# A cross-attention and quantized-GLU kernel whose instruction order comes from a planner: a margin for TensorE in the plan, four planned durations, and new due times

## The chip, the cores and the metric

The kernel runs on one core of a Trainium2 chip. The metric is the device time of one execution in microseconds (us); three runs of the kernel before gave 574.42, 576.3 and 575.2 us, median 575.2. A core has engines with an instruction stream each: TensorE (PE in the profile; its weight loads are PEld), VectorE (DVE), ScalarE (ACT), GpSimd (POOL) and SyncE (SP), which here issues all DMAs. The streams run side by side and meet only in semaphores, so an engine that waits holds up everything behind it in its own stream.

## The reference, cut to what matters

There are 8 batches of 512 rows with 256 features, and a context of 64 rows for each.

```python
def block(x, ctx):                       # x (8, 512, 256), ctx (8, 64, 256), float32
    y = normalized(x)
    y = layernorm(y + attention(y, y, y, causal=True), g1, beta1)
    y = layernorm(y + attention(y, ctx, ctx, causal=False), g2, beta2)
    h = relu(y @ w1 + b1)                # 256 -> 1024
    y = layernorm(y + h @ w2 + b2, g3, beta3)
    x = x + y
    z = fp4(normalized(x))               # blocks of 16, scale = max |.| / 6, grid 0 .. 6
    h = silu(z @ fp4(w_gate).T) * (z @ fp4(w_up).T)     # 256 -> 704
    return x + fp4(h) @ fp4(w_down).T
```

## The kernel before, in words

The work of a batch has five stages: self-attention (`self_attention`, stage 0), cross-attention (`cross_attention`, 1), the MLP (`mlp`, 2), gate and up products of the GLU (`glu`, 3) and its quantization and down product (`down` in `glu`, 4). Rows are tiled by 128, so a batch has four row tiles. Everything is in float32; a TensorE product therefore shows twice the number of matmul instructions.

The functions do not emit instructions. They call `plan.op(engine, cost, emit, reads, writes, ...)` with a planned duration in us and the buffers that the operation reads and writes. When all batches are described, `Plan.order` (line 192) plays a small list schedule: each of the five engines takes, whenever it is free in the plan, the ready operation with the smallest key, and the sequence found in this way is what is emitted, engine by engine. The plan's times are not in the program; only the order is.

- A key is the latest start that still meets a due time (`_keys`, line 153): the table `DUE` gives one due for each batch and stage, the nine rows being batches 0 to 7 and the constants' loads (columns, index -1). An operation takes the minimum of its own due and of the latest starts of all that follow it, less the hop (`HOP`, `NEXT`) and its cost. TensorE's operations of a batch are also chained to each other.
- `push` is added to a key. Loads of x and z get `-LOAD_EARLY`; the preparation of the quantized weights (`weights`) gets a large positive one. That preparation is described with batch 0 and stage 0, as are the loads of w1 and w2.
- An operation counts as ready when its last input has landed and a hop has passed, 0.25 us behind TensorE, 0.13 behind VectorE, 0.16 behind ScalarE.
- Buffers come from kinds with a number of homes (`plan.kind`) or a share of another kind's homes (`plan.share` with a quota). An operation that needs a home waits in the plan until one is free; in an ordered kind homes are given in the order of description.

Transposes go by TensorE and a ScalarE copy for the first batches (`BY_PRODUCTS`: 4, 2 and 1 batches for the three uses in `turned`), else by a split into 16-bit planes on ScalarE, a store to device memory and a transposing DMA (`turned_by_transfers`). `down` transposes by DMA too, but by TensorE in the last batch.

The lines that the steps below speak of: L358 and L366 load x and z; L448, L438, L439, L458 and L465 are a normalisation's statistics (VectorE) and power (GpSimd), L524 its result on ScalarE; L480, L488, L496, L503 are the statistics of the norms by sums, where L488 are the squares on ScalarE, each with an accumulator read behind it; L537 and L545 apply such a norm on VectorE. L419 are transposes on TensorE, L831 the copy of their result (turned) on ScalarE, L767 the causal scores, L778 their exponentials, L787 the causal select on GpSimd, L800 the causal products with the values, L806 and L807 the division. In cross-attention L867 copies the context's transpose (zT), L883 makes the keys' products, L896 copies them (kq), L900 turns them, L927 is the product with the values. L961 and L981 are the MLP's two products, L969 the relu between them. L1036 is gate and up, L1048 and L1055 silu and the product, L578 to L610 the fp4 quantization, L1071 the split into planes, L1116 the down product, L1126 the addition to x and L1133 the store. L743 loads the norms' vectors, L729 b1 (c_rows), L1149 writes the pads, L1156 and L1160 load w1 and w2. L381 clears part of hqT, L378 sets a column of z, both on GpSimd ahead of everything.

Of the kernel before, what the change touches and what calls it, by code (L numbers as in the profile page):

```python
# [19 lines left out]
P = 128  # L20
# [12 lines left out]
PE_PASS = 0.429 / 512  # L33
HOP = {"PE": 0.25, "DVE": 0.13, "ACT": 0.16, "POOL": 0.1, "SP": 0.1}

NEXT = {"PE": 0.0, "DVE": 0.11, "ACT": 0.11, "POOL": 0.0, "SP": 0.0}
TABLE = 1.29

# [2 lines left out]
TILED = 2.65  # L41

BY_PRODUCTS = (4, 2, 1)
LOAD_EARLY = 2191.0
DUE = [
    [-1877.0, 638.0, 1236.0, -86.0, 359.0],
    [-498.0, 1140.0, 299.0, -53.0, 352.0],
    [251.0, 920.0, -109.0, 452.0, 665.0],
    [2244.0, 599.0, -92.0, 754.0, 95.0],
    [1032.0, 759.0, 1302.0, 1127.0, 22.0],  # L50
    [818.0, -579.0, 119.0, -1108.0, 586.0],
    [771.0, -1583.0, 341.0, 621.0, 85.0],
    [127.0, -388.0, -430.0, -94.0, -1479.0],
    [-2334.0],
]


# [31 lines left out]
class Plan:  # L89
# [102 lines left out]
    def order(self):  # L192
        self._keys()
        now, events, tick = 0.0, [], 0
        waiting = {e: [] for e in HOP}
        free_at = dict.fromkeys(HOP, 0.0)
        table, out = None, []
        for o in self.ops:
            o.left, o.ready = len(o.pred), 0.0
            if not o.left:  # L200
                waiting[o.engine].append(o)
        running = {}
        while True:
            progress = True
            while progress:
                progress = False
                for e in HOP:
                    if free_at[e] > now:
                        continue
                    best = None  # L210
                    for o in waiting[e]:
                        if o.ready > now:
                            continue
                        switch = o.table is not None and o.table != table
                        rank = (o.key + (4.0 if switch else 0.0), o.serial)
                        if (best is None or rank < best[0]) and self._take(o, False):
                            best = (rank, o, switch)
                    if best is None:
                        continue
                    _, o, switch = best  # L220
                    self._take(o, True)
                    waiting[e].remove(o)
                    if o.table is not None:
                        table = o.table
                    end = now + o.cost + (TABLE if switch else 0.0)
                    free_at[e] = end
                    out.append((now, o))
                    landed = end + o.lag
                    heapq.heappush(events, (end, tick, "end", None))
                    heapq.heappush(events, (landed, tick, "landed", o))  # L230
                    tick += 1
                    for s in o.succ:
                        s.left -= 1
                        s.ready = max(s.ready, landed + (NEXT if s.engine == e else HOP)[e])
                        if not s.left:
                            waiting[s.engine].append(s)
                            heapq.heappush(events, (s.ready, tick, "ready", s))
                            tick += 1
                    progress = True
            if not events:  # L240
                break
            now = events[0][0]
            while events and events[0][0] <= now:
                _, _, what, o = heapq.heappop(events)
                if what == "landed":
                    heapq.heappush(events, (now + HOP[o.engine], tick, "free", o))
                    tick += 1
                elif what == "free":
                    for b in o.bufs:
                        b.users -= 1  # L250
                        if not b.users:
                            k = self.kinds[b.kind]
                            k["free"].append(b.home)
                            k["held"] -= 1
        assert len(out) == len(self.ops), "the plan does not end"
        self.span = now
        return out
# [3 lines left out]
def kernel(  # L261
# [22 lines left out]
    SZ = z.shape[1]  # L284
# [20 lines left out]
    def several(name, count, shape):  # L305
        return [fixed(f"{name}_{k}", shape) for k in range(count)]


    plan = Plan(due=DUE)
    plan.kind("x", several("x", 6, [P, NT, D]))  # L310

    y0_homes = several("y0", 2, [P, NT, D + 2])

    z_homes = several("z", 8, [P, D + 2])
    plan.kind("y0", y0_homes)
    plan.kind("z", z_homes)
    plan.kind("zT", several("zT", 6, [P, ND, SZ]))
    plan.kind("turned", several("turned", 3, [P, ND, S]), ordered=False)
    plan.share("y0T", "turned", 1)
    plan.share("yT", "turned", 3, ordered=False)  # L320
    plan.share("zqT", "turned", 3)
    plan.kind("e", several("e", 1, [P, NT * (NT + 1) // 2 * P]))
    plan.kind("r", several("r", 3, [P, NT, D]))
    plan.kind("kq", several("kq", 4, [P, S // 2]))
    plan.kind("xp", several("xp", 6, [P, NT, SZ]))
    plan.kind("xpT", several("xpT", 3, [P, NT // 2 * P]))
    plan.kind("hT", several("hT", 8, [P, S]))
    plan.kind("zq", several("zq", 1, [P, NT, D]))
    plan.kind("zm", several("zm", 2, [P, NT * D]), ordered=False)
    plan.kind("wide", several("h", 8, [P, NI * P]), ordered=False)  # L330
    plan.share("h", "wide", 5)
    plan.share("hm", "wide", 3)
    plan.share("wq", "wide", 7)
    hqT_homes = several("hqT", 3, [P, NI * P])
    plan.kind("hqT", hqT_homes)

    hd_homes = [dram.tile([P, 2, NI * P], U16, tag=f"hd_{k}", name=f"hd_{k}") for k in range(3)]
# [2 lines left out]
    plan.kind("rest", [rest_home])  # L340
    zd_homes = [dram.tile([NT, P, 2, D], U16, tag=f"zd_{k}", name=f"zd_{k}") for k in range(4)]
    plan.kind("zd", zd_homes, ordered=False)
    plan.kind("ln", several("ln", 12, [P, 48]), ordered=False)
    plan.kind("q", several("q", 6, [P, 3, 64]), ordered=False)
    plan.kind("rt", several("rt", 7, [P, 4]), ordered=False)
    banks = [psum.tile([P, 512], F32, tag=f"bank{k}", name=f"bank_{k}") for k in range(8)]
    plan.kind("bank", banks, ordered=False)

# [76 lines left out]
    def norm_stats(v, view, pairs):  # L425

        s = plan.buf("ln")

        def st(t):
            return s.ap[:, 6 * t : 6 * t + 6]  # L430

        def mv(t):
            return s.ap[:, 24 + 2 * t : 26 + 2 * t]

        def variances(ts_):
            lo, hi = ts_[0], ts_[-1] + 1
            for t in ts_:
                nc.vector.bn_aggr(mv(t), st(t))  # L438
            nc.vector.tensor_scalar(  # L439
                s.ap[:, 32 + lo : 32 + hi],  # L440
                s.ap[:, 24:32].rearrange("p (t k) -> p t k", k=2)[:, lo:hi, 1], EPS, None, ALU.add,
            )

        for ts_ in pairs:
            lo, hi = ts_[0], ts_[-1] + 1
            for t in ts_:
                plan.op(
                    "DVE", 0.33, lambda t=t: nc.vector.bn_stats(st(t), view(t)),  # L448
                    reads=[(v, t)], writes=[(s, ("st", t))],
                )  # L450
            plan.op(
                "DVE", 0.1 + 0.09 * len(ts_), lambda ts_=ts_: variances(ts_),
                reads=[(s, ("st", t)) for t in ts_],
                writes=[(s, ("var", lo))] + [(s, t) for t in ts_],
            )
            plan.op(
                "POOL", 1.05,
                lambda lo=lo, hi=hi: nc.gpsimd.tensor_tensor(  # L458
                    s.ap[:, 36 + lo : 36 + hi], s.ap[:, 32 + lo : 32 + hi], mhalf[:, lo:hi], ALU.pow
                ),  # L460
                reads=[(s, ("var", lo))], writes=[(s, ("rstd", t)) for t in ts_],
            )
            plan.op(
                "DVE", 0.15,
                lambda lo=lo, hi=hi: nc.vector.scalar_tensor_tensor(  # L465
                    s.ap[:, 40 + lo : 40 + hi],
                    s.ap[:, 24:32].rearrange("p (t k) -> p t k", k=2)[:, lo:hi, 0],
                    -1.0, s.ap[:, 36 + lo : 36 + hi], ALU.mult, ALU.mult,
                ),
                reads=[(s, ("rstd", t)) for t in ts_] + [(s, t) for t in ts_],  # L470
                writes=[(s, ("shift", t)) for t in ts_],
            )
        return s

    def sums_stats(v, view, s):
# [8 lines left out]
        )  # L484
        for t in range(NT):
            plan.op(
                "ACT", 0.52,
                lambda t=t: nc.scalar.activation(  # L488
                    squares, view(t), AF.Square, bias=s.ap[:, 24 + t : 25 + t],
                    accum_out=s.ap[:, 28 + t : 29 + t],  # L490
# [8 lines left out]
            reads=[(s, ("sq", t)) for t in range(NT)], writes=[(s, "var")],  # L499
        )  # L500
        plan.op(
            "POOL", 1.05,
            lambda: nc.gpsimd.tensor_tensor(s.ap[:, 36:40], s.ap[:, 32:36], mhalf, ALU.pow),  # L503
            reads=[(s, "var")], writes=[(s, ("rstd", t)) for t in range(NT)],
        )
# [241 lines left out]
    def self_attention(b, xs):  # L747
# [13 lines left out]
        for k in range(NT):  # L761
# [3 lines left out]
            def scores(k=k, n=n, sc=sc):  # L765
# [17 lines left out]
            )  # L783

            plan.op(
                "POOL", 0.35,
                lambda k=k: nc.gpsimd.affine_select(  # L787
                    out=e.ap[:, ds(start[k], P)], in_=e.ap[:, ds(start[k], P)],
                    compare_op=ALU.is_ge, fill=0.0, base=0, pattern=[[1, P]],
# [157 lines left out]
    def mlp(b, r, xs):  # L947
# [8 lines left out]
        for f in range(NF):  # L956
            hp, h = plan.buf("bank"), plan.buf("hT")

            def product(f=f, hp=hp):
# [5 lines left out]

            plan.op("PE", ND * pe(S), product, reads=[yT, ready["w1"]], writes=[hp], takes=[h])
            plan.op(
                "ACT", act(S, True),
                lambda f=f, hp=hp, h=h: nc.scalar.activation(  # L969
                    h.ap, hp.ap, AF.Relu, bias=b1_sb[:, f : f + 1]  # L970
                ),
# [188 lines left out]
        "SP", 5.2, lambda: nc.sync.dma_start(w2_sb, w2.rearrange("(c p) d -> p c d", p=P)),  # L1160
        writes=[ready["w2"]],
    )
    plan.push = 2035.0
    weights()
    plan.push = 0.0
    for b in range(B):
# [38 lines left out]
```

## Time and profile before

| What | Value |
|---|---|
| Median of 3 runs | 575.2 us (574.42 to 576.3) |
| The profiled execution, its own time | 576.26 us |
| Its span, first to last instruction | 574.5 us |
| Mean granted clock of TensorE | 1.000 |
| Costliest on TensorE: L1036, 512 matmuls | 157.5 us |
| L981, 512 matmuls | 112.6 us |
| L961, 256 matmuls | 112.5 us |
| L1116, 384 matmuls | 87.2 us |
| VectorE's costliest: L603 on h, 76 | 66.8 us |
| ScalarE's costliest: L488 on r, 96 | 48.7 us, 508 ns each |
| DMA traffic | 66.88 MB, mean 116 GB/s |

The page names an engine's busy time and its share of the span, then draws the span in 40 slices of 14.4 us, each digit a busy share in tenths (9 is 90% or more). The waits view adds up who waited for whom: the total, how often, the longest. The chain of work goes back from the last instruction to what released each step; in order of time a line is start, length, and what ran. A timeline line is start, duration, engine, line, operation, out<-in, shapes, count. Durations that overlap in an engine's pipeline are longer than the distance of two starts.

### The profile page before, as it was taken

The numbers are of one execution on the slowest core, as the hardware profiler recorded it, in microseconds if no ns is written. First come the engines' busy times: TensorE is split into PE (matmuls) and PEld (weight loads), VectorE is DVE, ScalarE is ACT, GpSimd is POOL, SyncE is SP. The second block draws the span as 40 slices with busy tenths as digits, with TensorE's granted clock in tenths as the row PEclk, the third lists the DMA queues.
The fourth block names the chain that finished last, engine by engine and source line by source line (L and its number), as shares of the span: only waits on it lengthen the run. The fifth ranks groups of instructions, "written<-read, shape, count | busy, mean of one in ns | idle before, by whom it ended". The sixth has DMA issues, their size and how long they took to land.

```text
span 574.5 us, 7037 instructions
## 1 busy us (share of the span) xinstructions
PE 563.8 (98%) x2209; PEld 391.2 (68%) x2209; DVE 447.8 (78%) x1125; ACT 361.8 (63%) x761; POOL 62.2 (11%) x93
## 2 busy tenths in 40 slices
PE   5999999999999999999999999999999999999997
PEld 2767584866747668658486667766765866877686
DVE  4789988869998865755259999978997656399892
ACT  4677869598887672791638558887845256364431
POOL 3521101011200120110101102210100000010000
PEclk9999999999999999999999999999999999999999
DMA  7770387246466513322023546585771421436501
GB/s 236 119 230 2 101 219 169 73 119 157 116 158 175 137 52 83 99 71 49 1 73 98 137 126 156 148 198 154 153 180 62 124 62 38 111 106 151 151 19 46
DMA packets 143220, 66.88 MB, mean 116 GB/s; under 512 B 107976, under 2 KB 142672, under 8 KB 143184
## 3 DMA queue, kind: packets, MB, share of 16 engines
q1 hardware_dynamic: 143184, 66.44, 45.4%
q8 instruction: 17, 0.28, 0.2%
q14 instruction: 19, 0.16, 0.1%
HBM read 10.42 MB, written 29.66 MB: 70 GB/s over the span
## 4 chain that ended last, share of the span: by engine, by line
PE 98%; ACT 1%; DMA 0%; SPq 0%; issue 0%; DVE 0%; ACTq 0%
PE bank L1036 27%; PE bank L981 19%; PE bank L961 19%; PE bank L1116 15%; PE bank L767 7%; PE bank L800 6%; PE bank L419 2%; PE bank L927 1%; PE bank L883 1%; DMA z<-in_ctx_dram 0%; ACT squares L488 0%; PE bank L900 0%; SPq L358 0%; ACT turned L831 0%; PE bank L1102 0%
## 5 line engine op out<-in xcount | busy, mean ns | idle before, releaser
L1036 PE MATMUL bank<-wgu,turned 128*128 128x352 f32 x512 | 157.5, 460 | 0.0
L1036 PEld LDWEIGHTS bank<-wgu,turned 128*128 128x128 f32 x512 | 96.3, 190 | 51.8 <-issue 1.7
L981 PE MATMUL bank<-w,hT 128*128 128x256 f32 x512 | 112.6, 379 | 0.0
L961 PE MATMUL bank<-turned,w 128*128 128x512 f32 x256 | 112.5, 593 | 0.0
L981 PEld LDWEIGHTS bank<-w,hT 128*128 128x128 f32 x512 | 97.0, 190 | 13.8
L1116 PE MATMUL bank<-wd,hqT 128*128 128x256 f32 x384 | 87.2, 380 | 0.0
L961 PEld LDWEIGHTS bank<-turned,w 128*128 128x128 f32 x256 | 48.2, 190 | 56.9 <-issue 51.7
L1116 PEld LDWEIGHTS bank<-wd,hqT 128*128 128x128 f32 x384 | 72.4, 190 | 14.2 <-issue 2.9
L503 POOL TENSOR_TENSOR ln<-ln,mhalf 128x4 f32<-128x4 f32 x32 | 37.7, 1180 | 352.0 <-DVE ln L496 352.0
L603 DVE SCALAR_TENSOR_TENSOR h<-h,h 128x704 f32<-128x704 f32 (+2 forms) x76 | 66.8, 883 | 3.8 <-ACT h L597 3.4
L488 ACT ACTIVATE squares<-r,ln 128x256 f32<-128x256 f32 x96 | 48.7, 508 | 32.0 <-DVE ln L480 29.7
L969 ACT ACTIVATE hT<-bank,cols 128x512 f32<-128x512 f32 x64 | 42.8, 681 | 21.7 <-PE bank L961 21.5
L1048 ACT ACTIVATE h<-bank 128x352 f32<-128x352 f32 x64 | 29.2, 460 | 36.4 <-PE bank L1036 32.5
L1071 ACT COPY h<-h 128x1408 uint16<-128x1408 uint16 x28 | 38.0, 1362 | 19.4 <-DVE h L610 17.9
L1055 DVE TENSOR_TENSOR h<-h,bank 128x352 f32<-128x352 f32 x64 | 32.4, 516 | 12.3 <-PE bank L1036 8.6
L992 DVE SCALAR_TENSOR_TENSOR r<-bank,r 128x256 f32<-128x256 f32 x32 | 13.5, 421 | 35.0 <-PE bank L981 34.7
L767 PE MATMUL bank<-turned 128*128 128x512 f32 (+3 forms) x128 | 39.8, 457 | 0.4 <-ACT turned L831 0.4
L597 ACT ACTIVATE h<-h 128x704 f32<-128x704 f32 (+2 forms) x38 | 29.7, 788 | 14.0 <-DVE h L591 13.9
L800 PE MATMUL bank<-y,e 128*128 128x258 f32 x160 | 36.8, 381 | 0.0
L800 PEld LDWEIGHTS bank<-y,e 128*128 128x128 f32 x160 | 30.1, 190 | 5.9 <-issue 1.0
L591 DVE SCALAR_TENSOR_TENSOR h<-h,q 128x704 f32<-128x704 f32 (+2 forms) x38 | 33.5, 883 | 0.2
L610 DVE TENSOR_TENSOR h<-h,q 128x704 f32<-128x704 f32 (+2 forms) x38 | 33.4, 879 | 0.2
(90 smaller groups left out, 639.9 us busy)
## 6 DMA issues: line engine op xcount, KB each, us to landing
zd<-zm SPq DMA_DIRECT2D x25, 512.0 KB, 3.0
hd<-h SPq DMA_DIRECT2D x30, 352.0 KB, 3.0
out_dram<-x SPq DMA_DIRECT2D x32, 128.0 KB, 1.7
x<-in_x_dram SPq DMA_DIRECT2D x7, 512.0 KB, 5.3
w<-in_L_xattn_w_dram SPq DMA_DIRECT2D x2, 1024.0 KB, 7.4
z<-in_ctx_dram SPq DMA_DIRECT2D x16, 64.0 KB, 4.6
zd<-h SPq DMA_DIRECT2D x2, 384.0 KB, 3.1
h<-in_L_ffn_w_down_dram SPq DMA_DIRECT2D x2, 352.0 KB, 4.2
```

The costliest lines, as they stand in the source:

```text
L488: lambda t=t: nc.scalar.activation(squares, view(t), AF.Square, bias=s.ap[:, 24 + t : 25 + t], accum_out=s.ap[:, 28 + t : 29 + t],),
L503: lambda: nc.gpsimd.tensor_tensor(s.ap[:, 36:40], s.ap[:, 32:36], mhalf, ALU.pow),
L591: lambda: nc.vector.scalar_tensor_tensor(blocks_of(view()), blocks_of(view()), TIE, each(rc()), ALU.mult, ALU.mult),
L603: lambda reverse=reverse, f=f: nc.vector.scalar_tensor_tensor(view(), mm(), LEAST, view(), ALU.max, f, reverse1=reverse),
L767: nc.tensor.matmul(sc.ap[:, :n], yT.ap[:, c, ts(k, P)], yT.ap[:, c, k * P :], start=(c == 0), stop=(c == ND - 1),)
L800: nc.tensor.matmul(av.ap[:, : D + 2], e.ap[:, ds(start[k] + (t - k) * P, P)], y0.ap[:, k, :], start=(k == 0), stop=(k == t),)
L961: nc.tensor.matmul(hp.ap, w1_sb[:, c, ts(f, P)], yT.ap[:, c, :], start=(c == 0), stop=(c == ND - 1),)
L969: lambda f=f, hp=hp, h=h: nc.scalar.activation(h.ap, hp.ap, AF.Relu, bias=b1_sb[:, f : f + 1]),
L981: nc.tensor.matmul(fp.ap[:, :D], hT[f].ap[:, ts(t, P)], w2_sb[:, f, :], start=(f == 0), stop=(f == NF - 1),)
L1036: nc.tensor.matmul(gp.ap[:, :HI], zT.ap[:, c, ts(t, P)], wgu[:, c, ds(j * I + n * HI, HI)], start=(c == 0), stop=(c == ND - 1),)
L1071: lambda: nc.scalar.copy(planes(), h.ap[:, :I].bitcast(U16).rearrange("p (k h) -> p h k", h=2)),
L1116: nc.tensor.matmul(op.ap[:, :D], hqT.ap[:, ts(c, P)], wd[:, c, :], start=(c == 0), stop=(c == NI - 1),)
```

## The change

In the plan, an operation of TensorE whose input comes from another engine counts as ready 0.3 us later than before (`MARGIN`). Four planned durations are others: a square on ScalarE 0.63 for 0.52, the relu `act(S) + 0.08` = 0.57 for `act(S, True)` = 0.68, the power on GpSimd 1.12 for 1.05, the causal select 0.44 for 0.35. The due times of all batches, LOAD_EARLY and the weights' push have new values, and some kinds have another number of homes: x 5 for 6, z 7 for 8, zT 7 for 6, xp 3 for 6, xpT 6 for 3, hT 9 for 8, hqT 4 for 3, ln 11 for 12, rt 6 for 7; y0T may hold 3 of the turned homes for 1, wq 8 of the wide ones for 7. What is computed, and with which instructions, stays.

```diff
--- before.py
+++ after.py
@@ -33,6 +33,8 @@
 PE_PASS = 0.429 / 512
 HOP = {"PE": 0.25, "DVE": 0.13, "ACT": 0.16, "POOL": 0.1, "SP": 0.1}
 
+MARGIN = 0.3
+
 NEXT = {"PE": 0.0, "DVE": 0.11, "ACT": 0.11, "POOL": 0.0, "SP": 0.0}
 TABLE = 1.29
 
@@ -41,17 +43,17 @@
 TILED = 2.65
 
 BY_PRODUCTS = (4, 2, 1)
-LOAD_EARLY = 2191.0
+LOAD_EARLY = 1700.0
 DUE = [
-    [-1877.0, 638.0, 1236.0, -86.0, 359.0],
-    [-498.0, 1140.0, 299.0, -53.0, 352.0],
-    [251.0, 920.0, -109.0, 452.0, 665.0],
-    [2244.0, 599.0, -92.0, 754.0, 95.0],
-    [1032.0, 759.0, 1302.0, 1127.0, 22.0],
-    [818.0, -579.0, 119.0, -1108.0, 586.0],
-    [771.0, -1583.0, 341.0, 621.0, 85.0],
-    [127.0, -388.0, -430.0, -94.0, -1479.0],
-    [-2334.0],
+    [-1877.0, 811.0, 1886.0, -99.0, 137.0],
+    [-928.0, 775.0, -2.0, -53.0, 390.0],
+    [25.0, 1141.0, -117.0, 450.0, 574.0],
+    [2061.0, 248.0, -91.0, 511.0, 218.0],
+    [819.0, 659.0, 1600.0, 1389.0, 6.0],
+    [1162.0, -143.0, 926.0, -413.0, 793.0],
+    [1110.0, -2125.0, -110.0, 538.0, -358.0],
+    [-315.0, -102.0, 396.0, 405.0, -822.0],
+    [-2414.0],
 ]
 
 
@@ -231,7 +233,8 @@
                     tick += 1
                     for s in o.succ:
                         s.left -= 1
-                        s.ready = max(s.ready, landed + (NEXT if s.engine == e else HOP)[e])
+                        hop = NEXT[e] if s.engine == e else HOP[e] + MARGIN * (s.engine == "PE")
+                        s.ready = max(s.ready, landed + hop)
                         if not s.left:
                             waiting[s.engine].append(s)
                             heapq.heappush(events, (s.ready, tick, "ready", s))
@@ -307,31 +310,31 @@
 
 
     plan = Plan(due=DUE)
-    plan.kind("x", several("x", 6, [P, NT, D]))
+    plan.kind("x", several("x", 5, [P, NT, D]))
 
     y0_homes = several("y0", 2, [P, NT, D + 2])
 
-    z_homes = several("z", 8, [P, D + 2])
+    z_homes = several("z", 7, [P, D + 2])
     plan.kind("y0", y0_homes)
     plan.kind("z", z_homes)
-    plan.kind("zT", several("zT", 6, [P, ND, SZ]))
+    plan.kind("zT", several("zT", 7, [P, ND, SZ]))
     plan.kind("turned", several("turned", 3, [P, ND, S]), ordered=False)
-    plan.share("y0T", "turned", 1)
+    plan.share("y0T", "turned", 3)
     plan.share("yT", "turned", 3, ordered=False)
     plan.share("zqT", "turned", 3)
     plan.kind("e", several("e", 1, [P, NT * (NT + 1) // 2 * P]))
     plan.kind("r", several("r", 3, [P, NT, D]))
     plan.kind("kq", several("kq", 4, [P, S // 2]))
-    plan.kind("xp", several("xp", 6, [P, NT, SZ]))
-    plan.kind("xpT", several("xpT", 3, [P, NT // 2 * P]))
-    plan.kind("hT", several("hT", 8, [P, S]))
+    plan.kind("xp", several("xp", 3, [P, NT, SZ]))
+    plan.kind("xpT", several("xpT", 6, [P, NT // 2 * P]))
+    plan.kind("hT", several("hT", 9, [P, S]))
     plan.kind("zq", several("zq", 1, [P, NT, D]))
     plan.kind("zm", several("zm", 2, [P, NT * D]), ordered=False)
     plan.kind("wide", several("h", 8, [P, NI * P]), ordered=False)
     plan.share("h", "wide", 5)
     plan.share("hm", "wide", 3)
-    plan.share("wq", "wide", 7)
-    hqT_homes = several("hqT", 3, [P, NI * P])
+    plan.share("wq", "wide", 8)
+    hqT_homes = several("hqT", 4, [P, NI * P])
     plan.kind("hqT", hqT_homes)
 
     hd_homes = [dram.tile([P, 2, NI * P], U16, tag=f"hd_{k}", name=f"hd_{k}") for k in range(3)]
@@ -340,9 +343,9 @@
     plan.kind("rest", [rest_home])
     zd_homes = [dram.tile([NT, P, 2, D], U16, tag=f"zd_{k}", name=f"zd_{k}") for k in range(4)]
     plan.kind("zd", zd_homes, ordered=False)
-    plan.kind("ln", several("ln", 12, [P, 48]), ordered=False)
+    plan.kind("ln", several("ln", 11, [P, 48]), ordered=False)
     plan.kind("q", several("q", 6, [P, 3, 64]), ordered=False)
-    plan.kind("rt", several("rt", 7, [P, 4]), ordered=False)
+    plan.kind("rt", several("rt", 6, [P, 4]), ordered=False)
     banks = [psum.tile([P, 512], F32, tag=f"bank{k}", name=f"bank_{k}") for k in range(8)]
     plan.kind("bank", banks, ordered=False)
 
@@ -454,7 +457,7 @@
                 writes=[(s, ("var", lo))] + [(s, t) for t in ts_],
             )
             plan.op(
-                "POOL", 1.05,
+                "POOL", 1.12,
                 lambda lo=lo, hi=hi: nc.gpsimd.tensor_tensor(
                     s.ap[:, 36 + lo : 36 + hi], s.ap[:, 32 + lo : 32 + hi], mhalf[:, lo:hi], ALU.pow
                 ),
@@ -484,7 +487,7 @@
         )
         for t in range(NT):
             plan.op(
-                "ACT", 0.52,
+                "ACT", 0.63,
                 lambda t=t: nc.scalar.activation(
                     squares, view(t), AF.Square, bias=s.ap[:, 24 + t : 25 + t],
                     accum_out=s.ap[:, 28 + t : 29 + t],
@@ -499,7 +502,7 @@
             reads=[(s, ("sq", t)) for t in range(NT)], writes=[(s, "var")],
         )
         plan.op(
-            "POOL", 1.05,
+            "POOL", 1.12,
             lambda: nc.gpsimd.tensor_tensor(s.ap[:, 36:40], s.ap[:, 32:36], mhalf, ALU.pow),
             reads=[(s, "var")], writes=[(s, ("rstd", t)) for t in range(NT)],
         )
@@ -783,7 +786,7 @@
             )
 
             plan.op(
-                "POOL", 0.35,
+                "POOL", 0.44,
                 lambda k=k: nc.gpsimd.affine_select(
                     out=e.ap[:, ds(start[k], P)], in_=e.ap[:, ds(start[k], P)],
                     compare_op=ALU.is_ge, fill=0.0, base=0, pattern=[[1, P]],
@@ -965,7 +968,7 @@
 
             plan.op("PE", ND * pe(S), product, reads=[yT, ready["w1"]], writes=[hp], takes=[h])
             plan.op(
-                "ACT", act(S, True),
+                "ACT", act(S) + 0.08,
                 lambda f=f, hp=hp, h=h: nc.scalar.activation(
                     h.ap, hp.ap, AF.Relu, bias=b1_sb[:, f : f + 1]
                 ),
@@ -1160,7 +1163,7 @@
         "SP", 5.2, lambda: nc.sync.dma_start(w2_sb, w2.rearrange("(c p) d -> p c d", p=P)),
         writes=[ready["w2"]],
     )
-    plan.push = 2035.0
+    plan.push = 4016.0
     weights()
     plan.push = 0.0
     for b in range(B):
```

## The prediction

> **What bounds the kernel now.** I read the page first, then TensorE's waits, then the chain of work in order of time, then the rows around the two waits that chain shows. The page:
>
> ```profile
> span 574.5 us, 7037 instructions
> ...
> PE 563.8 (98%) x2209; PEld 391.2 (68%) x2209; DVE 447.8 (78%) x1125; ACT 361.8 (63%) x761; POOL 62.2 (11%) x93
> ...
> PE   5999999999999999999999999999999999999997
> ...
> DVE  4789988869998865755259999978997656399892
> ```
>
> TensorE is busy in 563.8 of 574.5 us, and only the first and the last slice are not full. So the question is what an order of the same instructions can still win. TensorE's waits answer it:
>
> ```profile
> PE bank L419 <- DMA z<-in_ctx_dram: 5.6, 1, 5.6
> PE bank L419 <- ACT y L524: 0.9, 1, 0.9
> PE bank L900 <- ACT kq L896: 0.7, 1, 0.7
> PE bank L767 <- ACT turned L831: 0.4, 1, 0.4
> ```
>
> That is all of it: 7.6 us in four waits. The first is the start: x and ctx have to land. The second is the first normalisation. Asked from 15 us on, the same view keeps the last two, 0.7 + 0.4 = 1.1 us. Behind the last matmul lie 3.2 us (its end near 571.4, the span's end 574.5: an addition and the last store), which no order shortens. From 37 us to 571 us the chain is matmuls end to end, and the TensorE rows of the timeline show no wait in it.
>
> The chain also shows that some of the "busy" time at the start is not full speed. Two lines of the same 16 matmuls, batch 0's scores and a later batch's:
>
> ```profile
> 10.06 6.71 PE bank L767 x16
> ...
> 148.98 4.32 PE bank L767 x16
> ```
>
> The first took 6.71 - 4.32 = 2.39 us more. [...] (the 0.7 and 0.4 us waits did not slow the matmuls behind them).
>
> **What the two waits are made of.** ScalarE's timeline between 33 and 37 us:
>
> ```profile
> 35.12 0.51 ACT L488 ACTIVATE squares<-r,ln 128x256 f32<-128x256 f32 x1
> 35.54 0.19 ACT L488 ACTIVATION_READ_ACCUMULATOR squares<-r,ln 128x1 f32 x1
> 35.63 0.35 ACT L896 COPY kq<-bank 128x256 f32<-128x256 f32 x1
> 35.88 0.45 ACT L867 ACTIVATE zT<-bank 128x128 f32<-128x128 f32 x2
> 36.21 1.08 ACT L831 COPY turned<-bank 128x512 f32<-128x512 f32 x2
> ```
>
> Four squares with their accumulator reads stand ahead of the kq copy; they began at 33.21, 33.85, 34.49 and 35.12, so one occupies 0.63 us, where the plan has 0.52. The plan thought them done 4 x 0.11 = 0.44 us before they were. The keys that kq copies were out of TensorE at 34.8. So of the 0.72 us wait some 0.44 us is an error of the plan, and the 0.38 us wait for turned is queued behind the same copies.
>
> **The change part by part.** No instruction is added to the engines' work per batch; MARGIN is in the plan alone and costs nothing on the chip. What can change is the order on each engine.
>
> *Four durations.* Squares 0.52 to 0.63 (above: agrees with 0.63). Relu 0.68 to 0.57: its rows last 681 ns, but back to back on ScalarE they start 0.57 us apart. Pow 1.05 to 1.12: rows of 1180 ns (L503) and 999 ns (L458). Select 0.35 to 0.44: 447 ns. All nearer to the trace. Worth: the 0.44 us above at most in that place, 0 to 1.1 us in all, since only 1.1 us of waits is left after 15 us. Relu has cover either way: a product for it is four instructions, 1.72 us (32 of them are 13.73 us in the chain), three times its 0.57.
>
> *The margin.* An operation of TensorE whose input has just landed is passed over for one that has been ready for 0.3 us. Where ready work abounds (37 to 571 us) that only swaps matmuls, worth 0. Where it is scarce (before 37 us) it may put a filler ahead of an urgent one: from -0.4 us (turned's wait covered) to +0.5 us (a filler such as eight transposes, 1.04 us, half of it in the way). I take -0.1, near the low waits the trace has.
>
> *Dues.* A due reaches back: the plan takes the smallest of an operation's own due and those of all that follow it. So what counts for attention and MLP is the minimum over a batch's later stages. Before to after: batch 0 -86 to -99 (its first stage -1877 both times), batch 1 -53 both, batch 2 -109 to -117, batch 3 -92 to -91, batch 4 22 to 6. These are the same order. Batches 5 to 7 change (-1108 to -413, -1583 to -2125, -1479 to -822), but stay ahead of most others and are held back by buffers anyway. The weights' preparation has key -1877 + 2035 = 158 before and 2139 after: behind all attention and MLP both times. Taken as 0; its cover is the filled middle. In 500 to 560 us VectorE is busy 54.7 of 60 us (windows of 20 us: 17.86, 18.87, 17.95), so quantization pushed into the end would show from 5.3 us on.
>
> *Loads.* LOAD_EARLY falls by 491. An x load of batch 2 lies some 80 us of planned work ahead of its due: -109 - 80 - 2191 = -2380 before, ahead of the vectors' -2334; -117 - 80 - 1700 = -1897 after, behind their -2414. So on SP's queue the pads (2.56 us), c_rows (0.37) and seven vectors (about 3.2) move ahead of x of batches 2 to 4: these issue perhaps 7 to 9 us later, batch 2's near 14 us, landing 5.3 us later (DMA row) near 20. The vectors gain nothing: their first reader started at 25.67 and waited for no DMA. Batch 2's transposes run at 32.49; the normalisation before them costs 1.40 + 0.36 + 0.17 + 1.01 + 0.16 + 2.08 = 5.2 us, so x may land as late as 27.3. Cover 7 us: cost 0 if VectorE is free then, up to 3.3 us if it isn't (second rival).
>
> *Buffers.* x 6 to 5: one load less at the start. Before, six batches' statistics are on VectorE by 24 us; the sixth's 4 x 0.37 + 0.36 + 0.17 = 2.0 us leaves a stretch that is 17.2 of 20 us busy. Batch 5 must wait for batch 0's stores; before, its attention ran near 205 us and batch 0's last products near 236, so it has to move. There VectorE is 10.1 of 20 us busy (220 to 240), so other work can stand in: 0, within -0.5 and +2. The hqT clear grows from 3 to 4 (0.16 us of GpSimd), z's shrinks by one; GpSimd idled 1.8 us behind them until 4.27: 0. The other counts (y0T's share, xp, xpT, hT, zT, wq, ln, rt) set only when a buffer is free; I see no TensorE wait for one, so 0, with the same bounds.
>
> **Sum**, against the profiled execution (span 574.53, own time 576.26, so 1.73 us around it): -0.4 for the squares, -0.1 for the margin, -0.1 for the sixth batch's statistics: -0.6, so a span of 573.9 and 575.7 with what lies around. The median of the runs, 575.2, is 1.1 below the profiled one; the same -0.6 gives **574.6**.
>
> **Rivals.**
> 1. *Faster.* All waits but the loads' go: 0.85 + 0.72 + 0.38 = 1.95 us, 573.2[...]. For it: the errors corrected are the ones at these waits. Against: the 0.85 us wait hangs on batch 0's load and normalisation, whose order does not change.
> 2. *Slower: the statistics of batches 2 to 4 collide with the first normalisations.* Landing after 20 us instead of by 12, they bring 3 x 2.0 = 6.1 us of VectorE into 20 to 40 us, where it idles 2.8. The excess, 3.3 us, delays batch 0's and 1's normalisations, and TensorE has no MLP to fill in before 56.26: 575.2 + 3.3 = 578.5. It decides as soon as more than 2.8 us of them fall between 20 and 40 us. Against: the sixth batch's 2.0 us are gone from there, and 40 to 60 us has 1.7 us more.
> 3. *It doesn't do what it says.* The wait at kq goes and an equal one comes: 575.2.
>
> **How the numbers follow.** About 0.3% (1.7 us) is what a measurement of this kernel can tell from no change: 573.5 to 576.9. Likeliest case 0.42 (574.6), third rival 0.08 (575.2): within, 0.50. First rival 0.14: faster. Second, with whatever else breaks a packed TensorE, 0.36: slower. A reordered plan could also bring a 1.1 us pair of waits like the seen one to half of the eight batches: +4.4, and with part of rival 2 about +6. So the range is 573.0 to 581.0: half of the first rival and the outer third of the slower cases stay out. The likeliest case alone spans 573.6 to 575.8.
>
> **What would show it.** Right: TensorE's waits after 15 us under 1 us; kq's copy no longer behind four squares; vectors ahead of batch 2's x on SP; five batches' statistics early; the same 2209 matmuls. Wrong: TensorE waiting between 15 and 56 us for normalised rows or turned, or slices under 9 in the middle or near the end with VectorE full; or the 16 scores of batch 0 no longer at 6.7 us, which would be the clock and not the plan.

## The result and the profile after

The changed kernel takes 579.18 us in the median of 4 runs (579.1 to 580.61), the one before 575.02 us of 4 in the same comparison: ratio 1.0073, 95% interval 1.0052 to 1.0094. It is slower by 4.2 us where I had forecast 0.6 us faster. L numbers of the changed kernel are 3 higher than before (L896 is L899, L767 is L770, L961 is L964). Its page:

```profile
span 577.4 us, 7022 instructions
...
PE 565.5 (98%) x2209; PEld 391.5 (68%) x2209; DVE 445.2 (77%) x1125; ACT 361.4 (63%) x759; POOL 60.1 (10%) x93
...
PE   5989999999999999999999999999999999999997
...
PEclk9989999999999999999999999999999999999999
```

The middle and the end are as full as before. What is new stands in the third slice (29 to 43 us): TensorE under 9 tenths, and a granted clock under 9. TensorE's waits from 15 us on (who waited, total, times, longest), which were 1.1 us before:

```profile
PE bank L903 <- ACT kq L899: 1.5, 1, 1.5
PE bank L803 <- POOL e L790: 0.7, 1, 0.7
PE bank L770 <- ACT turned L834: 0.2, 1, 0.2
```

The wait at kq has doubled instead of shrinking, one for the causal select is new, 2.4 us in all. The windows of 10 us (length, then busy time and count of PE, PEld, DVE, ACT, POOL, then the clock) show what follows the longer one:

```profile
30.00:40.00 10.00, 8.48 (x44) 5.65 (x43) 9.06 (x42) 6.79 (x21) 2.50 (x3) 0.93 0.31 97
40.00:50.00 10.00, 10.00 (x53) 6.97 (x52) 8.99 (x33) 5.56 (x15) 2.06 (x5) 0.90 0.17 46
```

A clock of 0.93 and 0.90 loses 10 x 0.07 + 10 x 0.10 = 1.7 us. TensorE's timeline has it too: four score matmuls of 512 columns behind the wait take 2.82 us, where the same four took 1.99 before.

```profile
34.23 1.08 PE L886 MATMUL bank<-turned,zT 128*64 128x256 f32 x8
36.83 0.44 PE L903 MATMUL bank<-ident,kq 128*128 128x128 f32 x2 [1.52 <-ACT kq L899]
...
37.59 2.82 PE L770 MATMUL bank<-turned 128*128 128x512 f32 x4
```

The same lines show why the wait grew. TensorE makes the keys (L886, before L883), ScalarE copies them to kq, and TensorE reads the copy (L903, before L900). In the kernel before, other work of TensorE stands in this gap:

```profile
33.72 1.08 PE L883 MATMUL bank<-turned,zT 128*64 128x256 f32 x8
34.73 0.58 PE L419 MATMUL bank<-ident,z 64*128 64x64 f32 x6
```

From the end of the keys to the reading of kq it is 36.03 - 34.80 = 1.23 us before, of which the transposes of z fill 0.51, and 36.83 - 35.31 = 1.52 us after, of which nothing is filled. So of the 0.80 us by which the wait grew, 0.51 are work that now stands elsewhere, and 0.29 are a later copy.

Between the two profiled executions the account is: waits 2.4 - 1.1 = +1.3, clock +1.7, first matmul 5.26 instead of 5.56, -0.3: +2.7. The first MLP product starts at 59.01 instead of 56.26, +2.75, and the spans differ by 2.9: after 60 us hardly anything more is lost. Smaller terms of the start are left out of the sum, and that it fits to a tenth is in part luck. The medians differ by 4.2 because the profiled execution of before, 576.26, was 1.2 us above the median of this comparison, and that of the changed kernel was not.

SP's queue moved as forecast:

```profile
11.22 0.43 SPq L746 DMA_DIRECT2D v_beta<-in_L_xattn_beta_dram  x1
11.69 0.43 SPq L361 DMA_DIRECT2D x<-in_x_dram  x1
```

The vectors now go ahead of batch 2's x, and VectorE, with nothing to normalise, is idle for 6.85 us; then additions of beta3 to x (L560) stand between the divisions of batch 0:

```profile
17.67 0.17 DVE L809 RECIPROCAL rt<-bank 128x1 f32<-128x1 f32 x1 [6.85 <-PE bank L803]
...
19.38 1.10 DVE L560 TENSOR_TENSOR x<-x,v_beta 128x256 f32<-128x256 f32 x3
```

The chain of work that ended last leads through them in the changed kernel, from the landing of a vector over these additions, the divisions and the power of batch 0's norm to the select that is waited for, and from there to the squares and kq:

```profile
11.22 8.14 DMA v_beta<-in_L_xattn_beta_dram
19.38 1.10 DVE x L560 x3
...
27.43 0.46 POOL e L790
```

In the chain of before no such transfer stands behind the start. Runs e13 and e16 below take these additions out of it.

### The profile page after: what moved, and what is told of

Same layout as the page of the kernel before. It is cut to its first block, busy times and chain, and to the rows that moved or that the text cites. A ratio compares the mean times of both kernels' runs of the same rounds, so it can differ in the third digit from the quotient of the medians.

```text
span 577.4 us, 7022 instructions
## 1 busy us (share of the span) xinstructions
PE 565.5 (98%) x2209; PEld 391.5 (68%) x2209; DVE 445.2 (77%) x1125; ACT 361.4 (63%) x759; POOL 60.1 (10%) x93
## 4 chain that ended last, share of the span: by engine, by line
PE 94%; SPq 2%; DMA 1%; DVE 1%; ACT 1%; POOL 0%; issue 0%
PE bank L1039 26%; PE bank L984 19%; PE bank L964 19%; PE bank L1119 14%; PE bank L803 5%; PE bank L770 5%; PE bank L930 1%; PE bank L422 1%; DMA v_beta<-in_L_xattn_beta_dram 1%; PE bank L886 1%; SPq L746 0%; ACT squares L491 0%; SPq L369 0%; DVE x L560 0%; SPq L361 0%; PE bank L903 0%
## 5 line engine op out<-in xcount | busy, mean ns | idle before, releaser
L984 PE MATMUL bank<-w,hT 128*128 128x256 f32 x512 | 113.9, 380 | 0.0
L964 PE MATMUL bank<-turned,w 128*128 128x512 f32 x256 | 112.4, 593 | 0.0
L964 PEld LDWEIGHTS bank<-turned,w 128*128 128x128 f32 x256 | 48.3, 190 | 56.3 <-issue 51.0
L606 DVE SCALAR_TENSOR_TENSOR h<-h,h 128x704 f32<-128x704 f32 (+1 forms) x76 | 66.6, 880 | 5.0 <-ACT h L600 4.7
L770 PE MATMUL bank<-turned 128*128 128x512 f32 (+3 forms) x128 | 41.2, 471 | 0.2 <-ACT turned L834 0.2
L581 DVE TENSOR_REDUCE q<-h 128x44 f32<-128x704 f32 (+2 forms) x38 | 33.2, 875 | 2.0 <-DMA h<-in_L_ffn_w_down_dram 1.8
L770 PEld LDWEIGHTS bank<-turned 128*128 128x128 f32 x128 | 23.8, 202 | 15.6 <-issue 9.0
```

Source lines behind the costliest of these rows:

```text
L581: lambda: nc.vector.tensor_reduce(amax(), blocks_of(view()), AX.X, ALU.max, apply_absolute_value=True),
L606: lambda reverse=reverse, f=f: nc.vector.scalar_tensor_tensor(view(), mm(), LEAST, view(), ALU.max, f, reverse1=reverse),
L770: nc.tensor.matmul(sc.ap[:, :n], yT.ap[:, c, ts(k, P)], yT.ap[:, c, k * P :], start=(c == 0), stop=(c == ND - 1),)
L964: nc.tensor.matmul(hp.ap, w1_sb[:, c, ts(f, P)], yT.ap[:, c, :], start=(c == 0), stop=(c == ND - 1),)
L984: nc.tensor.matmul(fp.ap[:, :D], hT[f].ap[:, ts(t, P)], w2_sb[:, f, :], start=(f == 0), stop=(f == NF - 1),)
```

## Experiments

Two questions: where the 4 us come from in this order of instructions, and what in the change made this order. For the first I kept the changed kernel's planned sequence and moved single operations in it, or added idle work. For the second I planned anew with one part of the change. The code is cut to the lines that matter; helpers and the marks by which operations are found are left out. Times are medians; ratios are to the kernel before, on the same chip.

**The clock: e1, e4, e2.** e1 puts idle transposes where TensorE waits for kq:

```diff
         def scores():
+            if b == 0:
+                for _ in range(12):
+                    nc.tensor.transpose(sc.ap[:, 3 * P : 4 * P], ident, ident)
             for j in range(2):
```

> The changed kernel with 12 extra transposes of the identity (into an unused corner of a bank) put on TensorE ahead of batch 0's turned scores, where TensorE waits 1.5 us for the kq copy; the result is not touched. Theory A (that wait makes the array drop to half rate, and the slow matmuls from 38.5 to 42 us cost 1.7 us on top of the wait): granted clock back to 1.000, the causal scores there at 0.43 us apart instead of 0.85, span about 1.7 us shorter than the changed kernel's 577.4, so 575.7. Theory B (the slow stretch comes from the order or from DMA traffic, not from the wait): span 577.4 within 0.3.

577.18 us, 1.0039 [1.0025, 1.0052]; span 575.4 in the profiled run, clock 1.000 in five of six runs; the sixth has 0.997 and a span 1.8 us longer. The kq copy comes when it came before, only the array stays busy, and 2.0 us go. e4 is the converse, in the kernel before:

```diff
+        def copied():
+            if b == 0:
+                for _ in range(2):
+                    nc.scalar.copy(idle_to, idle_from)      # 128 x 320
+            nc.scalar.copy(kq.ap, keys.ap[:, : S // 2])
```

> The kernel before with two idle copies of 320 columns ahead of batch 0's kq copy on ScalarE (about 0.7 us of it), so that its wait of 0.7 us becomes 1.4 to 1.5. Nothing else moves. Theory A: the wait grows by 0.7, and the clock drops to half behind it: 0.7 + 1.7 = 2.4 us, 577.4 by the runs' median of 575.0, granted clock 0.997. Theory B: only the 0.7 us, 575.7, clock 1.000.

577.76 us, 1.0048 [1.0036, 1.0060], clock 0.997 in all five runs. Its TensorE timeline:

```profile
36.21 0.44 PE L909 MATMUL bank<-ident,kq 128*128 128x128 f32 x2 [1.57 <-ACT kq L903]
37.03 3.52 PE L769 MATMUL bank<-turned 128*128 128x512 f32 x4 [0.38 <-ACT turned L833]
```

With 0.85 us more of waiting the four matmuls behind it take 3.52 us instead of 1.99. Theory A (the wait brings the clock down) holds from both sides: with the wait of 1.57 us here the clock is 0.84 from 30 to 40 us and 0.99 from 40 to 50, where the kernel before has 1.00. That loses 1.7 us, about as much again as the wait. e2 moves the kq copy two squares forward, the step that I had hoped the planner would take:

```diff
+    seq = [o for _, o in plan.order()]
+    at = seq.index(kq_copies[0])
+    ahead = [i for i in range(at) if seq[i].engine == "ACT"][-2]
+    seq.insert(ahead, seq.pop(at))
```

> The changed kernel with batch 0's kq copy moved on ScalarE ahead of the last two of the four squares; all else in the same order. Theory A: the wait falls from 1.5 us to about 0.3, the clock stays up, so 1.2 + 1.7 = 2.9 us shorter: span 574.5. Theory B: only the wait is won, 576.2. A third possibility, the chain of batch 1's norm (its two squares come 0.3 us later) sets the start of the first MLP: 577 or more.

578.64 us, 1.0053 [1.0040, 1.0066]. The waits of e2 (L771 is turned's reader, L906 kq's):

```profile
PE bank L771 <- ACT turned L835: 1.0, 2, 0.8
...
PE bank L906 <- ACT kq L901: 0.5, 1, 0.5
```

kq's 1.5 us have become 0.5 at kq and 0.8 at turned, the copies that stand next on ScalarE (the other 0.2 at turned is an earlier wait, which the changed kernel has too). The clock stayed up in two of six runs (577.0 and 577.5 us) and fell in the four others (578.6 to 579.2). With the clock up, e2 stands where e1 does, so the move itself wins nothing that can be seen. Why the same order goes either way is not shown. A wait of 1.5 us had half rate behind it in the changed kernel and one of 1.6 us in e4; the last section sets a run beside them in which a wait as long had not.

**One part at a time: e3, e5 to e8, e17.**

```diff
-LOAD_EARLY = 1700.0                      # e3: in the changed kernel
+LOAD_EARLY = 2191.0
-MARGIN = 0.3                             # e5: in the changed kernel
+MARGIN = 0.0
+MARGIN = 0.3                             # e6: this and its use, in the kernel before
-"ACT", 0.52  "POOL", 1.05  "POOL", 0.35  act(S, True)      # e7: before
+"ACT", 0.63  "POOL", 1.12  "POOL", 0.44  act(S) + 0.08
```

e8 is the kernel before with the new DUE, LOAD_EARLY and push; e17 is the kernel before with the new numbers of homes and shares.

> The changed kernel with LOAD_EARLY back at 2191, which puts the x loads of batches 2 to 4 ahead of the pads and vectors on SP again; the whole plan is made anew with it. Theory L (the late loads empty VectorE between 11 and 17 us and crowd the first normalisations): VectorE busy about 7 of 10 us between 10 and 20 us again, first MLP product near 56.3 instead of 59.0, 575.2. Theory K (the order around kq, chosen by margin, durations and dues, is the cause, wherever the loads are): still a wait of over 1 us at kq and half rate behind it, 578 to 579.

> The changed kernel with MARGIN 0, all else as changed; planned anew. Theory M (the margin moves TensorE's fillers so that the kq copy falls behind four squares and the select behind the power): the waits after 15 us fall to about 1 us, granted clock 1.000, 575 to 576. Theory P (the dues and homes were fitted to one set of assumptions, and any single part taken alone gives a worse order): slower than the changed kernel, 580 or more, with waits after 60 us too. Theory D (dues and homes did it): 579, the same waits.

> The kernel before with MARGIN 0.3 alone. Theory M: waits of over 1 us after 15 us and granted clock 0.997, 577 to 579. Theory P: slower than that, 580 or more, with TensorE waiting at several places past 60 us. Theory D: no change, 575.2.

> The kernel before with the four planned durations alone. My prediction's step (truer squares shorten the wait at kq): 574.8, wait at kq under 0.4 us. Theory P: slower, 577 or more. Theories M and D: no change, 575.2.

> The kernel before with the changed DUE, LOAD_EARLY and push alone: margin, durations and homes as before. Theory D (the new dues and the later loads set the bad order of the first 60 us): 578 to 580, wait at kq over 1 us, VectorE idle between 11 and 17 us. Theory M: 575.2. Theory P: slower than 580, with waits spread over the run.

> The kernel before with the changed numbers of homes and shares alone. Theory P (dues, durations, margin and homes fit together and each part alone spoils the order): 580 or more, with waits past 60 us. My prediction's step (the homes only set when a buffer is free, 0 within -0.5 and +2): 574.7 to 577.2.

| Run | Median us | Ratio to before |
|---|---|---|
| e3 changed, LOAD_EARLY 2191 | 581.84 | 1.0114 [1.0101, 1.0127] |
| e5 changed, no margin | 597.51 | 1.0388 [1.0357, 1.0419] |
| e6 before, margin | 591.63 | 1.0273 [1.0249, 1.0298] |
| e7 before, four durations | 582.56 | 1.0124 [1.0095, 1.0154] |
| e8 before, dues and loads | 596.22 | 1.0359 [1.0329, 1.0390] |
| e17 before, homes | 597.95 | 1.0387 [1.0366, 1.0409] |

Every part alone is slower than all of them together (1.0073), and taking the margin out of the whole, or giving LOAD_EARLY its old value, is slower too: theory P (the parts fit only together). The waits show how. TensorE's in e17, from 60 us on, where neither kernel has any:

```profile
PE bank L961 <- DVE q L578: 4.6, 1, 4.6
PE bank L1036 <- DMA turned<-zd: 4.6, 1, 4.6
PE bank L419 <- ACT xp L890: 3.1, 1, 3.1
```

And in e7, whose planned durations are the truer ones, likewise from 60 us on:

```profile
PE bank L767 <- DMA turned<-zd: 1.7, 1, 1.7
PE bank L1116 <- DMA hqT<-hd: 0.9, 1, 0.9
PE bank L1036 <- DMA turned<-zd: 0.8, 1, 0.8
```

Long waits at few places, for other engines and for transfers. In e7 5.6 us of such waits have come past 15 us, and the wait at kq is gone, but not in the way that I had argued. The kq copy still stands behind a square, the last of four; TensorE has scores to do in the gap, and reads kq at 36.97:

```profile
35.35 0.51 ACT L488 ACTIVATE squares<-r,ln 128x256 f32<-128x256 f32 x1
...
35.86 0.35 ACT L896 COPY kq<-bank 128x256 f32<-128x256 f32 x1
```

```profile
35.21 1.56 PE L767 MATMUL bank<-turned 128*128 128x384 f32 x4
```

The margin alone goes the other way: in e6 kq waits 1.5 us, with four of the six transposes of z ahead of the keys' products instead of behind them. The homes alone (e17) do it too, 1.3 us with all six ahead. So more than one part can take the work out of this gap; which did it in the joint change is not shown.

e3 did not try what it was meant to: with the new due of the vectors, -2414, batch 2's x at -117 - 80 - 2191 = -2388 is still behind them on SP, as its timeline shows. What changed there is that x of batches 3 and 4 now goes ahead of w1 and w2.

**The place of the loads and the fillers (the additions of beta3): e9, e13, e16.** Moves in the changed kernel's own sequence:

```diff
+    seq = ahead_of("pads", [("x", 2), ("x", 3), ("x", 4)])        # e9, e16
+    seq = ahead_of(("divide", 0), [("st", 2)])                    # e9, e16
+    to = [o.tag for o in seq].index(("pow", 1))                   # e13, e16
+    fill = [o for o in seq[:to] if o.tag and o.tag[0] == "beta3"]
+    seq = [o for o in seq[:to] if o not in fill] + [seq[to]] + fill + seq[to + 1 :]
```

> The changed kernel's own order, with two moves only: on SP the x loads of batches 2 to 4 go ahead of the pads, c_rows and the vectors, and batch 2's statistics go ahead of batch 0's divisions on VectorE (and their power ahead of the rest on GpSimd). Theory L, the second rival (late loads empty VectorE from 11 to 17.7 us and crowd the first normalisations): VectorE busy over 5 of 10 us between 10 and 20, the two waits at the select and at kq down to 1 us together, no half rate at 38 us, span near 575. Theory K (the order on ScalarE and GpSimd around kq and the select makes the waits, not crowding on VectorE): both waits stay within 0.4 us, span 577.0 to 577.8.

580.41 us, 1.0092 [1.0068, 1.0116]. It told nothing of the loads: the vectors now came later, and the early L560 (here L566) held VectorE for its own:

```profile
22.54 1.10 DVE L566 TENSOR_TENSOR x<-x,v_beta 128x256 f32<-128x256 f32 x3 [3.17 <-DMA v_beta<-in_L_xattn_beta_dram]
```

> The changed kernel's own order with one move on VectorE: the twelve additions of beta3 to x of batches 0 to 2, which stand between batch 0's divisions and batch 1's norm (the first at 19.38 us, right as its vector lands), go behind batch 1's statistics. Theory F (these fillers crowd the first normalisations and so make the select late): batch 0's power starts by 25.6 instead of 26.24, the wait at the select under 0.3 us, kq's wait a little less, 576.5 to 578. Theory K (ScalarE's order of squares before kq, and GpSimd's of power before select, make them): both waits as before, 579.2.

580.05 us, 1.0074 [1.0061, 1.0087]. TensorE's waits past 15 us begin with

```profile
PE bank L907 <- ACT kq L903: 1.6, 1, 1.6
PE bank L934 <- ACT xpT L924: 1.5, 1, 1.5
...
PE bank L807 <- POOL e L794: 0.2, 1, 0.2
```

The fillers do make the select late: its wait is 0.2 us here, and 0.7 to 1.2 with them in place (changed kernel 0.7, e2 1.1, e1 1.2). But put elsewhere they come with a new wait for xpT of 1.5 us. kq's wait does not depend on them: it is 1.6 us without them.

> The changed kernel's own order with the loads of batches 2 to 4 and batch 2's statistics ahead, as in e9, and the twelve additions of beta3 behind batch 1's statistics, as in e13, so that no early instruction on VectorE waits for the vectors that now land later (3.2 us in e9). Theory L (the late loads, my second rival) in a clean form: waits at the select and at kq under 1 us together, 575 to 576.5. Against it (the order around kq on ScalarE and what follows on it is what counts, wherever the statistics are): kq's wait still 1.3 to 1.7 us, clock 0.997, 578 to 580.

579.64 us, 1.0079 [1.0059, 1.0100]. With the loads early and no wait for a vector:

```profile
PE bank L940 <- ACT xpT L930: 3.1, 1, 3.1
PE bank L913 <- ACT kq L909: 1.6, 1, 1.6
```

kq still waits 1.6 us. So the late loads are not what makes that wait, and moving them ahead wins nothing.

**The select: e10, e14.** The first select of batch 1 ahead of the power of batch 0's norm on GpSimd; e14 adds e1's transposes.

```diff
+    power, first = tags.index(("pow", 0)), tags.index(("select", 1))
+    seq.insert(first, seq.pop(power))
```

> The changed kernel's own order with one move: on GpSimd the first causal select of batch 1 goes ahead of the power of batch 0's norm. Theory K: TensorE's wait for the select (0.7 us) goes, batch 0's norm comes 0.3 to 0.5 us later; kq's wait of 1.5 us stays or grows, the clock still drops: 576.9 to 577.4. If the select's wait is only moved on to kq: 577.4.

577.71 us, 1.0046 [1.0031, 1.0060]. In the profiled run TensorE's waits past 15 us rose from 2.4 to 3.4 us (1.7 for selects in two waits, 1.5 at kq, 0.2 at turned) and the clock fell (0.92, 0.84 and 0.89 in the windows of 10 us from 20 to 50 us, which loses 3.5 us); it is the slowest of the six. The five others kept a clock of 1.000; their waits are not on record.

> The changed kernel's own order with both repairs: the first select of batch 1 ahead of the power, and 12 idle transposes in the wait at kq. If the clock is all that remains of the loss in the second run of this pair: granted clock 1.000 in nearly all runs and 576.5 to 577.2, as with the transposes alone or up to 0.7 us better. If the select's wait only moves: 577.2, no better than with the transposes alone.

577.38 us, 1.0029 [1.0019, 1.0038], clock 0.999 or 1.000 in all eight runs: no better than e1. The select's wait only moves.

**The start: e11, e12, e15**, in the kernel before. e12 also moves kq, as e2 does.

```diff
+    for _ in range(18):                                     # e11, e12, e15
+        nc.tensor.transpose(banks[7][:, :P], ident, ident)
     for _, o in plan.order():
...
+                for _ in range(keep[k] if keep else 0):     # e15: 5, 2, 2, 2 ahead of the
+                    nc.tensor.transpose(banks[7][:, :P], ident, ident)   # first four
```

> The kernel before with 18 transposes of the identity ahead of all work on TensorE (about 3.8 us at half rate, in the time in which it waits for ctx); the result is not touched. If half rate at the start ends by sustained work, as the trace's 6.71 against 4.32 us suggests, the array is up by 8 to 10 us instead of 12.5 to 14.3: 1.5 to 3 us shorter, 572.2 to 573.7 by median. If it doesn't, or if the transposes hold up the first real ones: 575.2 to 575.8.

575.59 us, 0.9999 [0.9991, 1.0007]: no difference. 4 of 13 runs had a span of 572.4 to 572.8 where the others had about 574, but the kernel before has two such groups in this comparison too (572.8 to 573.2 in 9 of 20 runs, 573.7 to 574.2 in 11). In the profiled run TensorE ran 35 matmuls between 10 and 20 us, where it ran 33 in the kernel before; in e15 below it ran 43, with 1.13 us of that stretch idle.

> The same with batch 0's kq copy ahead of the last two squares on ScalarE, the step that my prediction hoped the planner would take. If the wait there is made of the squares: another 0.4 to 0.8 us than with the transposes alone. If the norm behind the squares is as urgent: no difference.

577.14 us, 1.0031 [1.0020, 1.0043]: with kq moved, turned waits 1.5 us and the clock falls in all six runs (0.997 or 0.994). In the kernel before, too, the step I hoped for loses 1.5 us.

> The kernel before with the 18 idle transposes at the start and 5, 2, 2 and 2 more ahead of batch 0's first four transposes, where TensorE waits for normalised rows, so that it is busy without a gap from 1.4 us on. Theory W (only a stretch without waits ends half rate; the 1.1 us wait at 5.7 us was what kept the array slow with 18 alone): full rate from 5 to 9 us on, 571.5 to 573.5. Theory V (half rate at the start ends at 12.5 to 14.3 us whatever is done before): 575.2 to 576.

574.66 us, 0.9985 [0.9977, 0.9994], faster than both kernels by little. Its TensorE timeline:

```profile
8.89 4.58 PE L769 MATMUL bank<-turned 128*128 128x512 f32 x16
```

The 16 score matmuls, 6.79 us in this view of the kernel before, take 4.58. The select behind them now makes TensorE wait 1.1 us, which it did not before: on GpSimd the four selects start at 14.25, behind a power of the norms that takes 1.01 us. The two profiled runs differ by 2.1 us in span (572.4 and 574.5), the medians by 0.85, since the profiled run of before lay above its median.

## Why the prediction was wrong, point by point

*The reading of the bound* was right: a full TensorE, 1.1 us of waits to win, nothing past 60 us to gain or, as it came, to lose.

*The step that failed first: the squares, -0.4 us.* "So of the 0.72 us wait some 0.44 us is an error of the plan" took a wait for the error of one duration. The changed plan has the true duration and still put four squares ahead of kq; the wait is 1.5 us. A wait is how late the copy comes less the work that TensorE has meanwhile, and I had counted the first alone: 0.51 of the 0.80 us that came are lost work in the gap. Even in e7, the durations alone, the wait goes by work in the gap, with a square still just ahead of the copy. e2 and e12 make the hoped-for move directly: the wait goes to turned, next on the same engine (0.8 us in e2, 1.5 in e12). ScalarE had several urgent operations at once, and I had not asked what was late next.

*The term that was mis-sized: the cost of a wait.* I had priced a wait at its own length, since the waits of 0.7 and 0.4 us did not slow the matmuls behind them (four scores in 1.99 us, clock 1.00). Behind the wait of 1.5 us in the changed kernel the clock is at half rate for 3.41 us, from 38.60 to 42.02, and 2.0 of the 4.2 us are this term (e1, which fills the wait; e4 from the other side).

*The margin, taken as -0.1,* was priced from -0.4 to +0.5. Alone (e6) it costs 2.7%, and at this place the wait for kq grows from 0.7 to 1.5 us.

*Dues and homes, taken as 0.* "These are the same order" compared the dues' minima by eye. e8 (with loads and push) and e17 measured 3.6 and 3.9% for these parts alone. The size in the whole, 0.7%, is not that of the parts: as far as these runs tell they fit only together, and a list schedule answers a small change with another order everywhere. So adding a cost per edit was the wrong form of sum for this change; what could be bounded was the whole, from what a full TensorE leaves to win.

*The loads* moved as forecast, batch 2's x at 11.69 us (forecast near 14) with VectorE empty behind them. The second rival's time, 578.5, lies near the measured one, but its mechanism is not what runs show: e13 gives the fillers on VectorE 0.5 to 1.0 us, the select's wait; e16 denies that the loads make kq's. That its time came out near is luck. (Two slips in the working: 3 x 2.0 is 6.0, not 6.1, and behind the last matmul lie 3.1 us, not 3.2. Nothing hangs on them.)

*The first and third rivals* are refuted by the waits.

*Open:* why the joint change puts its slack just there. With the clock held, 2.0 us remain (e1). In e1's own trace 1.2 us at the select, 0.2 at turned and 1.5 filled with idle transposes, less the 1.1 of before, are 1.8 of them; the last 0.2 are within the noise. The select's wait is longer there than in the profiled run of the changed kernel (1.2 for 0.7), because TensorE came to it earlier (26.7 and 27.2) and still went on at the same time (27.86 and 27.92): in these two runs the quicker start is lost at the select.

## What to carry to other kernels

Where an order comes from a planner whose numbers fit only together, don't price the parts of a change one by one: any part alone may lose several per cent that the whole does not. Before you book a wait as a gain, read what the waiting engine has to do in the gap, and what stands next in the releaser's own queue: that was late next in e2 (0.8 us) and in e12 (1.5 us). And price a stall on a full TensorE with its clock: here idle work in a gap of 1.5 us won 2.0 us (e1, 577.18 us), as much as the moved copy did in the two runs of e2 that kept the clock (577.0 and 577.5 us).

## What the runs showed of the hardware that I had not expected

A wait of 1.5 to 1.6 us had half rate behind it in the changed kernel, e4 and e13, in all their runs by the granted clock (0.997 or less), and cost 1.7 to 2.0 us more where I can tell (the changed kernel's windows, e4, e1). In the profiled run of the changed kernel the stretch at half rate lasts from 38.60 to 42.02 us. Here it is with the 3.41 us ahead of it (length, TensorE's busy time and count, then the clock):

```profile
35.19:38.60 3.41, 1.89 (x11) 1.00 0.42 133
38.60:42.02 3.42, 3.42 (x8) 0.50 0.00 0
```

TensorE is idle for 1.52 us of the first, the wait for kq, and busy all through the second. The waits of 0.7 and 0.4 us of the kernel before cost no clock: it has 1.00 from 30 to 40 us and from 40 to 50. But the length of one wait does not decide it alone. In the profiled run of e16 kq waits 1.6 us too, between 30 and 40 us, and the clock stays (the windows of 10 us, as above):

```profile
30.00:40.00 10.00, 8.41 (x46) 5.59 (x45) 8.74 (x33) 5.50 (x18) 2.21 (x2) 1.00 0.32 84
40.00:50.00 10.00, 6.85 (x36) 5.17 (x36) 9.71 (x42) 4.92 (x11) 2.85 (x5) 0.83 0.16 46
```

It falls in the next 10 us, in which TensorE is idle for 3.15 us. In e17 kq waits 1.3 us, and the clock is 1.00 from 30 to 50 us. What decides is not shown: no run moved a wait in time on purpose, and why e2 fell in four of six runs stays open.

At the start, 18 idle transposes with a wait of 0.9 us for y behind them changed nothing in the median, 575.59 us (e11). With the waits between the first transposes filled as well, all 16 scores, from 8.89 us on, took 4.58 us instead of 6.79 (e15).
